# A graph layer on one core: the order of VectorE's two-input operations inside a pass of the main loop

## The chip, the cores and the metric

The kernel runs on 1 core of a Trainium2 chip. The metric is the device time of one execution in microseconds (us). Five engines work side by side, each with its own queue of instructions that it takes strictly in order: PE (TensorE), DVE (VectorE), ACT (ScalarE), POOL (GpSimd) and SP (SyncE, which here only issues transfers).

## The reference

A graph has 12,500 nodes with 128 features each and 200,000 edges (src, dst, weight), sorted by dst. Features are layer-normed and cut at zero. Each edge gets a score from its two ends; each node keeps the 16 edges with the highest scores, and sums their source rows with softmax weights:

```python
h = jnp.maximum(_layernorm(x, axis=-1), 0.0)
Qv = h @ W_Q.T;  Ku = h @ W_K.T
score = einsum('md,md->m', Qv[dst], Ku[src]) / sqrt(d) * exp(-edge_dt)
# rank of each edge among those of its dst, by score
keep = rank < 16
w = where(keep, exp(score - seg_max[dst]), 0)
alpha = w / denom[dst]
agg = segment_sum(alpha[:, None] * (h[src] @ W_msg.T), dst)
out = x + relu(h @ W_self.T + agg)
```

## The kernel before

A first stage norms all rows and writes them to a table in DRAM, h_tab. It also turns the edge lists into columns: idx_all (sources), dec_all (decay), pos_all (an edge's place among those of its node) and dlw (its node, counted from a window's start).

The edges are then cut into G = 112 groups of GC = 14 chunks of 128 edges. A group is worked on with NJ = 15 chunks, since its last node's edges may run into the next group's first chunk. Everything after the first stage happens in one loop, fully written out, with the order of every instruction fixed by hand (tc.manual_schedule): pass i takes one step of several groups at once, each at a different stage. A call at(g, stage) puts a stage of group g in place; what a queue holds follows the order of these calls, and semaphores do the rest.

The life of a group g, with the pass in which each step stands:

- **Gather** (let_go and gather, lines 406 and 395, pass g-2): 14 times, DVE copies two indices from idx_all to ix (line 414) and POOL issues an indirect DMA for each chunk (line 399) that fetches 128 rows of h_tab into hs. POOL does nothing else in the loop. There are 7 hs buffers and 4 of ix. more(k) is let_go for two chunks, k = 0 to 6.
- **places** (line 474, pass g-1, DVE): ow (line 477) marks each edge's node in a window of WN = 40, po (line 479) its slot of KM = 40. Each compares two inputs in SBUF and writes 128 x 600 numbers.
- **far_of, to_edges** (ACT, pass g-1): a matrix from nodes to edges. **q_out, q_parts** (ACT; DVE, line 460, 128 x 128, two inputs in SBUF): the query of each node in three bf16 parts.
- **q_to_edges** (PE, line 490, pass g, in four parts of 4, 4, 4 and 3 chunks; the first stands at the head of the pass) puts the queries on edges, in PSUM; **scores** (DVE, line 500, four parts) multiplies them with the gathered rows and sums, one instruction a chunk. The last chunk of a group is the first of the next one's gather.
- **scores_in_slots** (DVE, line 508, 128 x 600, sl from po and the scores, two inputs in SBUF), at the end of pass g.
- **slots_by_node** (PE, lines 513 and 515, pass g+1), node_by_slots: scores in a node's slots.
- **best** (DVE, lines 529 to 541, pass g+2): the 16 highest per node, some thirteen small operations. It reads the PSUM tile et that slots_by_node of the next group writes too, and stands behind it.
- **kept_to_edges** (PE), **on_edges** (DVE, lines 564 to 571): whether each edge is kept; mine (line 569) has one input in PSUM and one in SBUF.
- **weights** (DVE, pass g+3): kept (line 579) and alz (line 580, 128 x 600, from ow and kept, both in SBUF). **sums** (PE, line 590, two parts) multiplies alz with the gathered rows.
- **sums_turned** (PE, line 598), **products** (PE), **output** (DVE, line 610, pass g+5), **store** (SP). sums_turned writes the PSUM tile so, which output of the group before it reads.

So there are four operations of 128 x 600 with two inputs in SBUF in each pass: sl, alz, ow and po.

Of the kernel before, what the change touches and what calls it, by code (L numbers as in the profile page):

```python
# [58 lines left out]
def bc(ap, n):  # L59

    return ap.unsqueeze(2).to_broadcast([ap.shape[0], ap.shape[1], n])
# [7 lines left out]
def bm(ap, n):  # L69

    return ap.unsqueeze(1).to_broadcast([ap.shape[0], n, ap.shape[1]])
# [3 lines left out]
def gnn_layer(  # L75
# [310 lines left out]
    with tc.tile_pool(name="win", bufs=2) as win, tc.manual_schedule():  # L386
        chunks = [min(NJ, CH - GC * g) for g in range(G)]
# [18 lines left out]
        def let_go(g, k):  # L406

            j0, j1 = 2 * k, min(2 * k + 2, own[g])
            if j0 >= j1:
                return  # L410
            if k == 0:
                T[g]["ix"] = win.tile([P, GC], I32, name="ix", bufs=4)
            ix = T[g]["ix"]
            nc.vector.tensor_copy(ix[:, j0:j1], idx_all[:, GC * g + j0:GC * g + j1])  # L414
            gather(g, j0, j1, lambda j: ix[:, j:j + 1])
# [55 lines left out]
            nc.scalar.activation(T[g]["to_e"][:, 0:n], T[g]["far"][:, 0:n], AF.Relu, bias=1.0, scale=-1.0)  # L471


        def places(g):
            n = chunks[g]
            T[g]["ow"] = win.tile([P, NJ, WN], F32, name="ow", bufs=6)
            nc.vector.tensor_tensor(T[g]["ow"][:, 0:n, :], bm(slots, n), bc(dlw[:, g, 0:n], WN), op=OP.is_equal)
            T[g]["po"] = win.tile([P, NJ, KM], F32, name="po", bufs=5)
            nc.vector.tensor_tensor(T[g]["po"][:, 0:n, :], bm(slots, n),
                                    bc(pos_all[:, GC * g:GC * g + n], KM), op=OP.is_equal)  # L480
# [142 lines left out]
        def at(g, stage, *args):  # L623
            if 0 <= g < G:
                stage(g, *args)
# [4 lines left out]
        for i in range(-3, G + 6):  # L630
            at(i + 3, load_nodes)
            at(i + 2, load_dst)

            more = (lambda k: let_go(i + 2, k)) if 0 <= i < G - 2 else (lambda k: None)
            at(i, q_to_edges, 0)
            at(i - 5, output)
            at(i - 5, store)
            at(i - 3, weights)
            more(0)
            at(i - 4, sums_turned)  # L640
            at(i - 4, sums_turned_out)
            at(i + 1, q_out)
            at(i, q_to_edges, 1)
            at(i + 1, far_of)
            at(i - 1, slots_by_node)
            at(i + 1, places)
            more(1)
            at(i - 2, best)
            more(2)
            at(i - 2, sum_of_exps)  # L650
            at(i - 1, slots_out)
            at(i, q_to_edges, 2)
            at(i + 2, h_turned)
            at(i, scores, 0)
            more(3)
            at(i + 1, to_edges)
            at(i + 1, q_parts)
            at(i + 2, h_turned_out)
            at(i - 3, sums, 0)
            at(i - 2, kept_to_edges)  # L660
            at(i, scores, 1)
            more(4)
            at(i, q_to_edges, 3)
            at(i - 2, one_over_sum)
            at(i - 3, sums, 1)
            at(i, scores, 2)
            at(i - 2, on_edges)
            more(5)
            at(i - 4, products)
            at(i - 3, sums_out)  # L670
            at(i - 2, exps)
            at(i, scores, 3)
            at(i, scores_in_slots)
            more(6)
            at(i - 1, node_by_slots)
            at(i + 2, q_made)

# [180 lines left out]
```

## Time and profile before

| | |
|---|---|
| median of 3 runs | 2125.32 us (2122.5 to 2127.98) |
| the profiled execution: its own time | 2125.5 us |
| its span, first to last instruction | 2123.7 us |
| mean granted TensorE clock | 0.795 |
| busy share: POOL, DVE, PE, ACT | 73%, 70%, 62%, 30% |

The busy share counts an engine's instructions; time in which it issues or waits is left out. The profile comes as a page (busy shares, costliest groups of instructions with what ended the idle time before them) and as answers of the trace: waits, the timeline of an engine, and busy time in chosen stretches. A line as `L477` is line 477 of the kernel, `out<-in` are names of its tiles, and `xcount` is how often.

### The profile page before, as it was taken

What the parts mean: (1) busy time and instruction counts of PE and PEld (TensorE: products, weight loads), DVE (VectorE), ACT (ScalarE), POOL (GpSimd) and SP (SyncE); (2) the same over time, 40 slices, a digit from 0 to 9 for tenths busy, and PEclk for the clock granted to TensorE, in tenths of its full rate; (3) what the DMA queues carried; (4) which work ended last, traced back from release to release, by engine and by line L of the source; (5) the groups of instructions that cost most, each with busy time, mean ns of one, the idle gap of its engine ahead of it and who ended that gap; (6) DMA issues with size and microseconds to landing.
All of it is one profiled execution on the core that took longest, in us unless ns stands there. A gap on an engine that the chain in (4) does not pass through costs nothing. (4 is left out here: it accounts for less than half of the span.)

```text
span 2123.7 us, 43559 instructions
## 1 busy us (share of the span) xinstructions
PE 1312.0 (62%) x14574; PEld 1210.1 (57%) x14575; DVE 1488.2 (70%) x7474; ACT 626.7 (30%) x1225; POOL 1544.1 (73%) x1585
## 2 busy tenths in 40 slices
PE   1166666666666666666666666666666666666665
PEld 1155566555555655555555656565666666565654
DVE  7667677777776777767777767677777776777764
ACT  3442222222222222222222222222222222222220
POOL 1477777777777777777777777777777777777773
PEclk9977877877777877877777777777777787877787
DMA  8453343333343343333333334334433343333420
GB/s 220 146 162 116 119 120 119 120 119 119 120 119 119 116 122 115 115 112 119 118 119 119 119 119 120 119 119 120 120 119 120 119 120 120 119 119 119 120 67 24
DMA packets 118805, 253.18 MB, mean 119 GB/s; under 512 B 33030, under 2 KB 76297, under 8 KB 118558
## 3 DMA queue, kind: packets, MB, share of 16 engines
q1 hardware_dynamic: 67336, 144.92, 19.7%
q0 software_dynamic: 50144, 102.74, 19.1%
q10 hardware_dynamic: 1094, 2.69, 0.5%
q8 instruction: 115, 1.88, 0.4%
q14 instruction: 116, 0.95, 0.1%
HBM read 236.40 MB, written 14.40 MB: 118 GB/s over the span
## 5 line engine op out<-in xcount | busy, mean ns | idle before, releaser
L399 POOL DMA_INDIRECT hs<-h_tab,ix x1535 | 1495.9, 975 | 467.8 <-issue 335.9
L500 DVE SCALAR_TENSOR_TENSOR prod<-hs,dec_all,q 128x128 f32<-128x128 f32 x1674 | 516.9, 345 | 334.3 <-DMA hs<-h_tab,ix 319.1
L490 PE MATMUL q<-q,to_e 128*128 128x128 bf16 x5022 | 464.2, 254 | 33.1 <-DVE prod L500 32.3
L598 PE MATMUL s<-ident,agn 128*128 128x128 f32 x112 | 49.3, 440 | 662.2 <-DVE kept L579 661.7
L490 PEld LDWEIGHTS <-to_e 128*128 128x128 bf16 x5022 | 410.1, 116 | 56.0 <-issue 39.8
L590 PE MATMUL a<-hs,alz 128*128 128x128 f32 x3348 | 425.8, 281 | 0.8 <-DVE alz L580 0.8
L598 PEld LDWEIGHTS s<-ident,agn 128*128 128x128 f32 x112 | 20.2, 180 | 678.4 <-issue 676.7
L590 PEld LDWEIGHTS a<-hs,alz 128*128 128x128 f32 x3348 | 404.4, 197 | 1.2 <-DVE alz L580 1.1
L515 PE MATMUL e<-ow,sl 128*41 128x40 f32 x3348 | 251.3, 265 | 8.4 <-DVE sl L508 8.4
L515 PEld LDWEIGHTS e<-ow,sl 128*41 128x41 f32 x3348 | 235.7, 184 | 23.6 <-DVE sl L508 9.2
L466 ACT ACTIVATE far<-dstb,nb 128x1920 bf16<-128x1920 int32 x112 | 212.9, 1901 | 5.1 <-DMA dstb<-in_dst_dram 5.1
L471 ACT ACTIVATE to_e<-far 128x1920 bf16<-128x1920 bf16 x112 | 201.2, 1796 | 0.1
L602 ACT COPY aggT<-s 128x128 f32<-128x128 f32 x112 | 29.8, 266 | 507.8 <-PE s L598 507.8
L529 DVE TENSOR_SCALAR ell<-slots,e 128x40 f32<-128x40 f32 x112 | 28.3, 253 | 205.3 <-PE e L515 192.6
L546 ACT ACTIVATE e<-v,km 128x16 f32<-128x16 f32 x112 | 34.4, 308 | 363.5 <-DVE km L538 363.5
L500 DVE DVE_READ_ACCUMULATOR prod<-hs,dec_all,q 128x1 f32 x1674 | 139.1, 83 | 0.2
L414 DVE COPY ix<-idx_all 128x2 int32<-128x2 int32 (+1 forms) x768 | 132.7, 173 | 0.0
L575 ACT ACTIVATE up<-up 128x15 f32<-128x15 f32 x112 | 24.1, 215 | 336.5 <-DVE up L567 336.4
L595 ACT ACTIVATE agn<-a,rden 128x128 f32<-128x128 f32 x112 | 41.2, 368 | 209.8 <-PE a L590 209.8
L508 DVE TENSOR_TENSOR sl<-po,s 128x600 f32<-128x600 f32 x112 | 87.5, 781 | 3.9
L580 DVE TENSOR_TENSOR alz<-ow,kept 128x600 f32<-128x600 f32 x112 | 87.5, 781 | 3.8
L399 POOL DMA_INDIRECT hs<-h_tab,idx_all x28 | 33.7, 1203 | 77.6 <-DMA x_end<-zpad 69.4
(150 smaller groups left out, 1562.7 us busy)
## 6 DMA issues: line engine op xcount, KB each, us to landing
dstb<-in_dst_dram SPq DMA_DIRECT2D x111, 960.0 KB
hs<-h_tab,ix POOLq DMA_INDIRECT x1535
h_r<-h_tab SPq DMA_DIRECT2D x112, 64.0 KB
x_t<-in_x_dram SPq DMA_DIRECT2D x108, 64.0 KB
out_dram<-o SPq DMA_DIRECT2D x108, 64.0 KB
xg<-in_x_dram SPq DMA_DIRECT2D x10, 560.0 KB
h_tab<-xg SPq DMA_DIRECT2D x10, 560.0 KB
dst_r<-in_dst_dram ACTq DMA_DIRECT2D x1, 803.2 KB
```

Of the source, the lines that this page charges most:

```text
L399: nc.gpsimd.indirect_dma_start(out=T[g]["hs"][:, j, :], out_offset=None, in_=h_tab[0:N, :], in_offset=bass.IndirectOffsetOnAxis(ap=index(j ...
L414: nc.vector.tensor_copy(ix[:, j0:j1], idx_all[:, GC * g + j0:GC * g + j1])
L466: nc.scalar.activation(T[g]["far"][:, 0:n], T[g]["dstb"][:, 0:n], AF.Square, bias=nb[:, g:g + 1])
L471: nc.scalar.activation(T[g]["to_e"][:, 0:n], T[g]["far"][:, 0:n], AF.Relu, bias=1.0, scale=-1.0)
L490: nc.tensor.matmul(pq[:, (j - j0) * P:(j - j0 + 1) * P], lhsT=T[g]["to_e"][:, j * P:(j + 1) * P], rhs=upper(T[g]["q"][:, k, :]), start=(k ...
L500: nc.vector.scalar_tensor_tensor(prod, rows_of(g, j), dec_all[:, c:c + 1], T[g]["pq", b][:, (j % 4) * P:(j % 4 + 1) * P], op0=OP.mult, op1 ...
L508: nc.vector.tensor_tensor(sl1[g % 2][:, 0:n, 0:KM], T[g]["po"][:, 0:n, :], bc(T[g]["s"][:, 0:n], KM), op=OP.mult)
L515: nc.tensor.matmul(et[0:KM + 1, STEP * j:STEP * j + WN], lhsT=sl1[g % 2][:, j, :], rhs=T[g]["ow"][:, j, :], start=False, stop=(j == n - 1))
L580: nc.vector.tensor_tensor(alz[g % 2].rearrange("e (j w) -> e j w", w=WW + STEP)[:, 0:n, 0:WN], T[g]["ow"][:, 0:n, :], bc(kept[:, 0:n], WN) ...
L590: nc.tensor.matmul(T[g]["pa"][:, 0:P], lhsT=alz[g % 2][:, WW * j + PRE:WW * j + PRE + P], rhs=rows_of(g, j), start=(j == 0), stop=(j == n ...
L595: nc.scalar.activation(T[g]["agn"], T[g]["pa"][:, 0:P], AF.Copy, scale=T[g]["rden"])
L598: nc.tensor.transpose(so[:, 2 * P:3 * P], T[g]["agn"], ident)
```

## The change

Stages of VectorE change their places inside a pass; places is cut into two stages, nodes_of (ow) and places (po). Each stage keeps its pass and its instructions.

```diff
-        def places(g):
+        def nodes_of(g):
             n = chunks[g]
             T[g]["ow"] = win.tile([P, NJ, WN], F32, name="ow", bufs=6)
             nc.vector.tensor_tensor(T[g]["ow"][:, 0:n, :], bm(slots, n), bc(dlw[:, g, 0:n], WN), op=OP.is_equal)
+
+        def places(g):
+            n = chunks[g]
             T[g]["po"] = win.tile([P, NJ, KM], F32, name="po", bufs=5)
...
             at(i - 5, output)
             at(i - 5, store)
-            at(i - 3, weights)
             more(0)
             at(i - 4, sums_turned)
             at(i - 4, sums_turned_out)
...
             at(i, q_to_edges, 1)
             at(i + 1, far_of)
             at(i - 1, slots_by_node)
-            at(i + 1, places)
+            at(i - 2, best)
             more(1)
-            at(i - 2, best)
-            more(2)
+            at(i - 3, weights)
             at(i - 2, sum_of_exps)
             at(i - 1, slots_out)
             at(i, q_to_edges, 2)
             at(i + 2, h_turned)
             at(i, scores, 0)
-            more(3)
+            more(2)
+            at(i + 1, nodes_of)
             at(i + 1, to_edges)
             at(i + 1, q_parts)
             at(i + 2, h_turned_out)
             at(i - 3, sums, 0)
             at(i - 2, kept_to_edges)
             at(i, scores, 1)
-            more(4)
+            more(3)
+            at(i + 1, places)
             at(i, q_to_edges, 3)
             at(i - 2, one_over_sum)
             at(i - 3, sums, 1)
             at(i, scores, 2)
+            more(4)
             at(i - 2, on_edges)
             more(5)
             at(i - 4, products)
             at(i - 3, sums_out)
             at(i - 2, exps)
             at(i, scores, 3)
+            more(6)
             at(i, scores_in_slots)
-            more(6)
```

## The prediction

> **What bounds the kernel now.** I read the page first, then the waits, then the timelines of POOL and VectorE (DVE) over two passes, then busy time by stretches of a pass. The chain that ended last holds only four pieces of the tail and says nothing of the loop. From the page, the groups (count | busy us, mean ns | idle before, releaser):
>
> ```profile
> L399 POOL DMA_INDIRECT hs<-h_tab,ix x1535 | 1495.9, 975 | 467.8 <-issue 335.9 <-DVE prod L500 34.1 <-DMA hs<-h_tab,ix 31.1
> L500 DVE SCALAR_TENSOR_TENSOR prod<-hs,dec_all,q 128x128 f32<-128x128 f32 x1674 | 516.9, 345 | 334.3 <-DMA hs<-h_tab,ix 319.1
> L529 DVE TENSOR_SCALAR ell<-slots,e 128x40 f32<-128x40 f32 x112 | 28.3, 253 | 205.3 <-PE e L515 192.6 <-issue 12.8
> ```
>
> POOL's 1535 gathers take 1495.9 us, and the idle time before them is in small pieces. From the waits (total us, times, longest):
>
> ```profile
> POOL hs L399 <- issue: 343.8, 1128, 0.3
> DVE prod L500 <- DMA hs<-h_tab,ix: 319.1, 399, 2.6
> ```
>
> POOL's longest gap is 0.3 us: it never runs dry. DVE, on the other hand, waits 319 us for gathered rows. So POOL sets the pace, with 14 gathers in a pass. From POOL's timeline (start us, us, engine):
>
> ```profile
> 1004.32 0.94 POOL L399 DMA_INDIRECT hs<-h_tab,ix  x1 [0.30 <-issue]
> 1005.56 1.54 POOL L399 DMA_INDIRECT hs<-h_tab,ix  x1 [0.30 <-issue]
> 1007.41 0.94 POOL L399 DMA_INDIRECT hs<-h_tab,ix  x1 [0.30 <-issue]
> 1024.88 1.08 POOL L399 DMA_INDIRECT hs<-h_tab,ix  x1 [0.30 <-issue]
> ```
>
> An undisturbed gather takes 0.94 and the next starts 0.30 later, so 1.248 a gather and 14 x 1.248 = 17.47 us a pass. Some gathers last longer. DVE's timeline around the first of them:
>
> ```profile
> 1003.18 0.35 DVE L500 SCALAR_TENSOR_TENSOR prod<-hs,dec_all,q 128x128 f32<-128x128 f32 x1 [0.72 <-DMA hs<-h_tab,ix]
> 1003.57 0.79 DVE L508 TENSOR_TENSOR sl<-po,s 128x600 f32<-128x600 f32 x1
> 1004.34 0.28 DVE L610 SCALAR_TENSOR_TENSOR o<-s,x_t 128x128 f32<-128x128 f32 x1
> 1004.74 0.78 DVE L580 TENSOR_TENSOR alz<-ow,kept 128x600 f32<-128x600 f32 x1
> 1005.51 0.78 DVE L477 TENSOR_TENSOR ow<-slots,dlw 128x600 f32<-128x600 f32 x1
> 1006.20 0.78 DVE L479 TENSOR_TENSOR po<-slots,pos_all 128x600 f32<-128x600 f32 x1
> 1009.03 0.25 DVE L529 TENSOR_SCALAR ell<-slots,e 128x40 f32<-128x40 f32 x1 [1.94 <-PE e L515]
> 1010.99 0.16 DVE L414 COPY ix<-idx_all 128x2 int32<-128x2 int32 x1
> 1024.37 0.77 DVE L479 TENSOR_TENSOR po<-slots,pos_all 128x600 f32<-128x600 f32 x1
> ```
>
> The gather at 1005.56 starts 0.05 into ow (L477) and lasts 0.60 too long: it goes on at 1006.16, which is ow's start + 0.65. The one at 1024.88 starts 0.51 into a po (L479), lasts 0.14 too long and goes on at po's start + 0.65. I went through the other long gathers of the loop in the same way: nearly all start inside the first 0.65 us of one of the four 600-element operations with two SBUF inputs (sl, alz, ow, po), and all that start inside it are held to its end. An operation that covers only the later part of a gather costs nothing, and DVE's four are 0.77 to 0.79 whatever POOL does. L569 and L571, as long but with one SBUF input, hold none.
>
> Over 103 passes of the loop the holds are 0.445 us a pass: 65 passes lose 0.5 to 0.7, 32 lose about 0.14 to 0.3, a few others lie between or above. That is all the change can win on POOL: 0.445 x 108 passes = 48 us (the group row gives the same size: 1535 x (975 - 944, the median) = 47.6).
>
> **The change part by part.** No instruction is added or removed. Per pass it moves kept/alz (L579, L580) from before best to behind it, ow (L477) behind scores 0, po (L479) behind scores 1, the second pair of index copies behind best, and the last one ahead of sl. None of it is issued by PE, ACT, SP or POOL, so those four keep their order; the index copies come up to some 4 us later within a pass, but they feed subset i+2 while the rows of subset i are awaited, at least 14 gathers ahead, and POOL does not notice.
>
> DVE's own path. From the output (1004.34) to best (1009.03) is 4.69 us, set by PE: the output frees the bank, then PE runs the transpose, 12 matmuls and slots_by_node. Today 2.76 of it is covered by alz, ow and po; afterwards only by one copy, so best's wait grows from 1.94 to about 4.3. Behind best stands the rest of the pass: best with its copy 2.03, kept and alz 0.90, scores 0 and copy 1.15, ow 0.69, q parts 0.53, scores 1 and copy 1.14, po 0.69, one over the sum 0.26, scores 2 and copy 1.15, on_edges and copy 2.09, scores 3 and copy about 1.0, sl 0.70: 12.3. With 4.69 that is 17.0 a pass, below POOL's 17.47. So DVE's added wait is paid from its waits for rows (3.1 us in the pass shown, about 0.5 to 1 left) and costs nothing; without that cover it would cost 2.4 x 108 = 260 us. PE gets alz about 3 us later relative to the output, waits some 2 us ahead of sums, and still ends about 4 us before the next output, out of the 6 it has.
>
> What decides is therefore where the four operations fall against gathers. The last product of a pass (1003.18) waits for a gathered row and so ties DVE's clock to POOL's in every pass. I walk the new order through the pass shown. sl stays at 1003.57. The output follows it directly, 0.70 later: 1004.27; best 4.69 later: 1008.96; alz after 1.96 + 0.07 + 0.20: 1011.19; ow after 0.70 + 1.08 + 0.07: 1013.04; po after 0.69 + 0.53 + 1.07 + 0.07: 1015.40. Gathers without the old hold start at 1005.57, 1006.82, 1008.06, 1009.31, 1010.56, 1011.81. The last is 0.62 into alz: held 0.03. The next starts at 1013.09, 0.05 into ow: held 0.60. Then 1014.94 and 1016.19, on either side of po. Sum 0.63, where before it was 0.60.
>
> This is no accident of one pass. ow now starts 1.85 after alz, and a gather released by alz starts again 0.65 + 1.248 = 1.90 after alz started, 0.05 into ow; one that just missed alz lands later in ow, by as much. So the pair takes 1.248 minus the gather's place after alz's start, about anything from 0 to 1.25, mean 0.62. With the row arriving 0.07 later against POOL (the passes that now lose only 0.14) the same walk gives 0.70. So with best at 4.69 the holds are about 0.65. Where TensorE's clock rises early, best comes early and each 0.1 us takes 0.1 off: 26 of the 103 passes have best at 4.30 to 4.65 (walk: 0.25 to 0.6). From the busy times by stretch (us, PE, PEld, DVE, ACT, POOL busy, then granted clock, DMA):
>
> ```profile
> 1004.34:1009.03 4.69, 4.26 (x46) 3.82 (x47) 2.72 (x10) 2.23 (x3) 3.78 (x4) 0.50 0.41 107
> 1016.51:1022.50 5.99, 0.00 (x1) 0.00 (x0) 4.24 (x19) 0.21 (x1) 4.47 (x6) 0.79 0.21 55
> ```
>
> PE runs up to best at a granted clock of 0.50, after 6 us of idling; with the idle time split into 2 and 4 the clock may be up in more passes. I take 45 to 75% of the passes at 0.65 and the others at 0.35 to 0.40: 0.51 to 0.575, so 0.545. Against 0.445 that is +0.10 x 108 = +10.8 us on the profiled execution's own 2125.5 (span 2123.7, 1.8 around it; the median of the runs, 2125.32, is the same within 0.2): 2136.
>
> [...]
>
> **The rivals.** *Fewer holds* (faster). The place is the distance from output to best: if PE's clock is up in most passes and its mean falls to 4.44 or less, alz has moved by a quarter and the sum of holds drops below 0.385. For it: PE's long idle time is cut. Against it: 77 of 103 passes now have 4.69, and about 4 us of idling remain. At a mean of 4.2 to 4.3 the holds are 0.15 to 0.25: 2125.5 - 0.245 x 108 = 2099; with none left, 2077.
>
> *The same sum, elsewhere*: holds of 0.39 to 0.50, 2120 to 2131, centre 2125. For it: the walk of the pass shown differs by 0.03 only.
>
> *Two whole holds a pass* (slower by far): best earlier than 4.05, so that alz catches a gather at its beginning and ow another: 0.9 to 1.2, +0.6 x 108, 2190. Or DVE's own 17.0 is short by over a microsecond and binds. Against both: best has not been below 4.29 in these passes, and DVE's parts are all measured.
>
> **How the numbers follow.** Likeliest case (holds 0.50 to 0.75, 2131 to 2158): 0.55. Same sum: 0.20. Fewer holds: 0.18. Two holds or DVE bound: 0.07. A measurement of this kernel tells about 0.3% (6.4 us) from no change, so slower by more is 0.62, within it 0.20, faster 0.18. The range leaves out most of the last case and the far part of fewer holds: 2106 (holds 0.26) to 2162 (holds 0.78).
>
> **What would show it.** Right: L399's mean at 980 to 985 ns instead of 975; long gathers starting inside ow, none inside po; best's wait for L515 up from 193 to over 400 us, products' wait for rows down to about 100; alz starting 7 us after the output. Wrong: a mean near 950 (fewer holds) or over 1000 (two holds); gaps on POOL over 0.3; products that no longer wait for rows (DVE binds).

## The result, and the profile after

The changed kernel takes 2151.64 us (median of 4 runs, 2148.46 to 2154.96), the kernel before 2123.91 beside it: ratio 1.0138, 95% interval 1.0123 to 1.0152. It is slower, as forecast, but by 27.7 us where 10.8 were forecast. The profiled execution took 2151.43, its span is 2149.7: 25.9 us over the span before. (In twelve of the eighteen experiment runs the kernel before, run beside them, itself took 2784 to 2800 us instead of some 2122; these twelve are kept apart below.)

The same three groups of the page as before the change (count | busy us, mean ns | idle before, releaser; lines behind 477 stand three lower in the changed file, so L500 is now L503):

```profile
L399 POOL DMA_INDIRECT hs<-h_tab,ix x1535 | 1514.2, 986 | 467.8 <-issue 316.1
...
L503 DVE SCALAR_TENSOR_TENSOR prod<-hs,dec_all,q 128x128 f32<-128x128 f32 x1674 | 501.4, 344 | 136.8 <-DMA hs<-h_tab,ix 125.5
...
L532 DVE TENSOR_SCALAR ell<-slots,e 128x40 f32<-128x40 f32 x112 | 30.7, 274 | 448.3 <-PE e L518 445.7
```

The gathers' idle time is the same to the digit (467.8) and their busy time is 18.3 us longer. VectorE's waits changed places as forecast: rows 319.1 to 125.5, best 192.6 to 445.7. From the waits (total us, times, longest):

```profile
PE s L601 <- DVE ix L414: 369.3, 105, 5.8
...
POOL hs L399 <- issue: 323.7, 1062, 0.3
...
PE a L593 <- DVE alz L583: 217.1, 112, 3.1
```

POOL's longest gap in the loop is still 0.3: no new wait stands in its way. PE waits about 2 us a pass for alz (217.1 / 112) and still 3.5 for the output (369.3 / 105; the index copy that this row names stands right behind the output, L613). POOL's timeline in two passes:

```profile
1002.98 0.94 POOL L399 DMA_INDIRECT hs<-h_tab,ix  x1 [0.30 <-issue]
1004.23 1.52 POOL L399 DMA_INDIRECT hs<-h_tab,ix  x1 [0.30 <-DVE prod L503]
1006.05 0.94 POOL L399 DMA_INDIRECT hs<-h_tab,ix  x1 [0.30 <-issue]
...
1021.03 0.94 POOL L399 DMA_INDIRECT hs<-h_tab,ix  x1 [0.30 <-issue]
1022.28 1.38 POOL L399 DMA_INDIRECT hs<-h_tab,ix  x1 [0.30 <-DVE ix L414]
```

and VectorE's, of which the two-input operations, the output and the head of best are shown:

```profile
1002.30 0.78 DVE L583 TENSOR_TENSOR alz<-ow,kept 128x600 f32<-128x600 f32 x1
...
1004.15 0.78 DVE L477 TENSOR_TENSOR ow<-slots,dlw 128x600 f32<-128x600 f32 x1
...
1006.52 0.77 DVE L482 TENSOR_TENSOR po<-slots,pos_all 128x600 f32<-128x600 f32 x1
...
1013.52 0.28 DVE L613 SCALAR_TENSOR_TENSOR o<-s,x_t 128x128 f32<-128x128 f32 x1
...
1017.89 0.34 DVE L532 TENSOR_SCALAR ell<-slots,e 128x40 f32<-128x40 f32 x1 [4.01 <-PE e L518]
...
1020.23 0.78 DVE L583 TENSOR_TENSOR alz<-ow,kept 128x600 f32<-128x600 f32 x1
...
1022.07 0.78 DVE L477 TENSOR_TENSOR ow<-slots,dlw 128x600 f32<-128x600 f32 x1
```

In the first pass the gather at 1002.98 starts 0.68 into alz, just past its 0.65, and runs free. The next starts 0.08 into ow and is held to ow's start + 0.65, as before the change: 1004.23 + 1.52 is ow's start + 1.60. In the second, best came 4.37 behind the output instead of 4.69; everything behind it is earlier by as much, so the gather falls 0.21 into ow and is held 0.44. Over the loop ow holds 103 gathers (51.3 us; 67 and 38.1 before), alz 49 (5.9), sl 15 (2.1), and po 4 instead of 36.

Where the 25.9 us stand: the last gather ends at 2103.35 instead of 2085.48, 17.9 later, which is the gathers' longer busy time. The other 8.1 stand in the tail, from there to the end of the span: 46.3 us instead of 38.3. The prediction had nothing there.

### The profile page after: what moved, and what is told of

Same layout as the page of the kernel before. It is cut to its first block, busy times and chain, and to the rows that moved or that the text cites. A ratio compares the mean times of both kernels' runs of the same rounds, so it can differ in the third digit from the quotient of the medians.

```text
span 2149.7 us, 43561 instructions
## 1 busy us (share of the span) xinstructions
PE 1427.9 (66%) x14574; PEld 1307.2 (61%) x14575; DVE 1465.7 (68%) x7474; ACT 624.4 (29%) x1225; POOL 1561.2 (73%) x1585
## 5 line engine op out<-in xcount | busy, mean ns | idle before, releaser
L399 POOL DMA_INDIRECT hs<-h_tab,ix x1535 | 1514.2, 986 | 467.8 <-issue 316.1
L593 PE MATMUL a<-hs,alz 128*128 128x128 f32 x3348 | 531.9, 323 | 217.1 <-DVE alz L583 217.1
L593 PEld LDWEIGHTS a<-hs,alz 128*128 128x128 f32 x3348 | 489.4, 232 | 241.7 <-DVE alz L583 241.7
L503 DVE SCALAR_TENSOR_TENSOR prod<-hs,dec_all,q 128x128 f32<-128x128 f32 x1674 | 501.4, 344 | 136.8 <-DMA hs<-h_tab,ix 125.5
L493 PE MATMUL q<-q,to_e 128*128 128x128 bf16 x5022 | 469.4, 256 | 9.7 <-DVE prod L503 9.6
L493 PEld LDWEIGHTS <-to_e 128*128 128x128 bf16 x5022 | 407.8, 117 | 25.1 <-issue 10.8
L532 DVE TENSOR_SCALAR ell<-slots,e 128x40 f32<-128x40 f32 x112 | 30.7, 274 | 448.3 <-PE e L518 445.7
L601 PE MATMUL s<-ident,agn 128*128 128x128 f32 x112 | 45.5, 406 | 378.7 <-DVE ix L414 369.3
L518 PE MATMUL e<-ow,sl 128*41 128x40 f32 x3348 | 245.3, 262 | 8.3 <-DVE sl L511 8.3
L518 PEld LDWEIGHTS e<-ow,sl 128*41 128x41 f32 x3348 | 229.8, 180 | 23.1 <-DVE sl L511 9.1
L503 DVE DVE_READ_ACCUMULATOR prod<-hs,dec_all,q 128x1 f32 x1674 | 138.3, 83 | 0.2
L399 POOL DMA_INDIRECT hs<-h_tab,idx_all x28 | 33.0, 1178 | 77.9 <-DMA x_end<-zpad 69.7
L574 DVE TENSOR_REDUCE kept<-mine 128x15 f32<-128x600 f32 x112 | 86.9, 776 | 3.8
```

The source lines that it names most:

```text
L399: nc.gpsimd.indirect_dma_start(out=T[g]["hs"][:, j, :], out_offset=None, in_=h_tab[0:N, :], in_offset=bass.IndirectOffsetOnAxis(ap=index(j ...
L493: nc.tensor.matmul(pq[:, (j - j0) * P:(j - j0 + 1) * P], lhsT=T[g]["to_e"][:, j * P:(j + 1) * P], rhs=upper(T[g]["q"][:, k, :]), start=(k ...
L503: nc.vector.scalar_tensor_tensor(prod, rows_of(g, j), dec_all[:, c:c + 1], T[g]["pq", b][:, (j % 4) * P:(j % 4 + 1) * P], op0=OP.mult, op1 ...
L518: nc.tensor.matmul(et[0:KM + 1, STEP * j:STEP * j + WN], lhsT=sl1[g % 2][:, j, :], rhs=T[g]["ow"][:, j, :], start=False, stop=(j == n - 1))
L574: nc.vector.tensor_reduce(kept[:, 0:n], mine[:, 0:n, :], axis=AX.X, op=OP.add)
L593: nc.tensor.matmul(T[g]["pa"][:, 0:P], lhsT=alz[g % 2][:, WW * j + PRE:WW * j + PRE + P], rhs=rows_of(g, j), start=(j == 0), stop=(j == n ...
```

## The experiments

The theory on trial is the prediction's: gathers set the pace, and a two-input operation of VectorE costs as much as the gather that starts inside its first 0.65 us loses. Rivals: VectorE's or TensorE's own path through a pass became longer (the bare wait ahead of best); or it is the distance between the four operations that counts, not their place against gathers.

**Where to read the loop's time.** The profiled execution of each run that could be compared (us):

| kernel | L399 busy (x1535) | last gather ends | tail behind it | span |
|---|---|---|---|---|
| before | 1495.9 | 2085.5 | 38.3 | 2123.7 |
| changed | 1514.2 | 2103.4 | 46.3 | 2149.7 |
| l0, before's order, light TensorE | 1494.7 | 2083.0 | 35.3 | 2118.3 |
| l5, in the gaps, light TensorE | 1455.6 | 2042.4 | 35.2 | 2077.6 |
| e5d, in the gaps | 1455.1 | 2043.4 | 39.8 | 2083.2 |
| e1d, weights back | 1465.3 | 2054.1 | 40.4 | 2094.4 |
| e4b, spare reduce ahead of alz | 1510.6 | 2101.4 | 48.3 | 2149.7 |
| e3b, spare reduce late | 1517.9 | 2106.2 | 49.5 | 2155.7 |

The second column less the first is 587 to 591 us in all eight, while the gathers' busy time covers 63 us and TensorE's work more than a factor of two; the gathers' idle time is 467.7 or 467.8 in each. So up to the last gather, what differs between these kernels is their gathers' own time, and the rest is the tail.

**l0_before_order: is it TensorE?** The order of before, with most of TensorE's products cut to one matmul for each group of them; best then comes 2.63 behind the output instead of 4.63. One of the cuts:

```diff
-            for j in range(n):
-                nc.tensor.matmul(et[0:KM + 1, STEP * j:STEP * j + WN], lhsT=sl1[g % 2][:, j, :],
-                                 rhs=T[g]["ow"][:, j, :], start=False, stop=(j == n - 1))
+            nc.tensor.matmul(et[0:KM + 1, 0:WW], lhsT=upper(sl1[g % 2][:, 0, :]),
+                             rhs=T[g]["to_e"][:, 0:WW], start=True, stop=True)
```

> A base for the runs that follow, the kernel before with TensorE's work cut from some 145 to 12 matmuls a pass (one bf16 matmul for each part of q_to_edges, one for slots_by_node, sums, products, h_turned, two for kept_to_edges, q_made left out), so that the values are no longer those of the layer. Every instruction of VectorE, GpSimd, ScalarE and SyncE and the order of all of them is that of the kernel before. On the chips that serve these calls the kernel before takes 2790 to 2800 us, since TensorE issues single matmuls about 1 us apart while gathers run and POOL waits for it; 12 matmuls a pass leave it room. Theory H: POOL sets the pace again, 14 gathers of 1.248 us and a hold of about 0.45 us a pass, nearly all under ow: 2110 to 2135 us, VectorE waiting for rows in each pass. Rival D (DVE's own path): with TensorE short, DVE's 13.1 us a pass bind: well under 1900. If TensorE's stalls still bind: over 2200, and the base is of no use.

Measured: 2121.47 us beside 2122.65, ratio 0.9995 (0.9986 to 1.0005). From the page (busy us (share) xinstructions, and the gathers):

```profile
PE 515.1 (24%) x1405; PEld 159.6 (8%) x1406; DVE 1490.3 (70%) x7474; ACT 615.4 (29%) x1225; POOL 1543.2 (73%) x1586
...
L401 POOL DMA_INDIRECT hs<-h_tab,ix x1535 | 1494.7, 974 | 467.7 <-issue 318.2
```

TensorE's busy time fell from 1312 to 515 us, and the time stayed. In before's order alz, ow and po stand ahead of best, so best's earlier coming moves none of them, and the holds stay as well (974 ns, 975 before). TensorE is not what the loop waits for.

**l5_in_gaps: the same cut, the four operations put beside gathers' starts.** ow and po go behind the first four of the seven index copies of a pass, with two of the products between them, so that each operation starts shortly after a gather has (e5's order):

```diff
             at(i - 3, weights)
             more(0)
+            more(1)
+            more(2)
+            more(3)
...
-            at(i + 1, places)
-            more(1)
+            at(i + 1, nodes_of)
+            at(i, scores, 0, 0, 2)
+            at(i + 1, places)
             at(i - 2, best)
...
-            at(i, scores, 0)
+            at(i, scores, 0, 2, 4)
```

> The same cut of TensorE's work, with ow and po in the gaps between gather starts (four index copies between alz and ow, two products of scores 0 between ow and po; alz at 1.56, ow at 2.54, po at 3.77 us behind the last product, gather starts at about 2.4, 3.6 and 4.9). Theory H: holds of 0 to 0.05 us a pass instead of about 0.45, so 40 to 50 us below the base with the old order; mean of a gather 945 to 950 ns against about 976. Rival D: the base within 5 us, since DVE's work is the same. Rival A (how far apart the operations stand): the base less 0 to 15 us, since the gaps between three of them are 0.3 to 0.5 us only.

Measured: 2080.07 us beside 2122.65, ratio 0.9804 (0.9788 to 0.9821), and 41.4 below l0; the gathers' mean (L401 there) is 948 ns. The holds are 0.04 us a pass.

**e5d_in_gaps: that order in the whole kernel.**

> The whole layer with ow and po in the gaps between gather starts. Where the kernel before takes about 2123: theory H 2074 to 2090, holds of 0 to 0.05 us a pass; rivals D and A 2110 to 2124. Where the kernel before takes about 2790, TensorE's stalls decide and the time says nothing.

Measured: 2085.69 us beside 2120.81, ratio 0.9836 (0.982 to 0.9853). It beats both kernels, with the same operations. The group of gathers, then VectorE's and POOL's timelines:

```profile
L399 POOL DMA_INDIRECT hs<-h_tab,ix x1535 | 1455.1, 948 | 467.8 <-issue 311.8
```

```profile
1002.15 0.78 DVE L511 TENSOR_TENSOR sl<-po,s 128x600 f32<-128x600 f32 x1
...
1003.37 0.78 DVE L583 TENSOR_TENSOR alz<-ow,kept 128x600 f32<-128x600 f32 x1
...
1004.37 0.77 DVE L477 TENSOR_TENSOR ow<-slots,dlw 128x600 f32<-128x600 f32 x1
...
1005.60 0.77 DVE L482 TENSOR_TENSOR po<-slots,pos_all 128x600 f32<-128x600 f32 x1
```

```profile
1002.87 0.94 POOL L399 DMA_INDIRECT hs<-h_tab,ix  x1 [0.30 <-issue]
1004.11 0.94 POOL L399 DMA_INDIRECT hs<-h_tab,ix  x1 [0.30 <-issue]
1005.36 0.94 POOL L399 DMA_INDIRECT hs<-h_tab,ix  x1 [0.30 <-issue]
1006.61 0.94 POOL L399 DMA_INDIRECT hs<-h_tab,ix  x1 [0.30 <-DVE po L482]
```

The gathers start 0.72 into sl, 0.74 into alz, 0.99 into ow and 1.01 after po began: none in the first 0.65. Each operation lies across the later part of a gather, and none is held; over the loop the holds are 0.06 us a pass. The four stand within 3.45 us, closer than in the changed kernel and nearly as close as before the change (2.63), where they cost 0.445 a pass. So distance between them is not what counts; their place against gathers is.

**e1d_weights_back: one part of the change undone.** In the changed kernel, weights returns to its place behind the output; ow and po stay behind scores 0 and 1.

```diff
             at(i - 5, store)
+            at(i - 3, weights)
             more(0)
...
             at(i - 2, best)
             more(1)
-            at(i - 3, weights)
```

> The changed kernel with kept and alz back behind the output and ow and po left apart behind best. Where the kernel before takes about 2123: theory H 2085 to 2105 (alz at 1.49 and, with best at 4.69, ow at 8.96 and po at 11.33 all miss; passes with an early best lose up to 0.56); rival D 2054 to 2124; rival A 2130 to 2150. Where the kernel before takes about 2790, it says nothing.

Measured: 2092.98 us beside 2120.81, ratio 0.9867 (0.985 to 0.9883): this part of the change alone takes a slowdown of 1.4% to a gain of 1.3%.

```profile
L399 POOL DMA_INDIRECT hs<-h_tab,ix x1535 | 1465.3, 955 | 467.8 <-issue 299.9
```

At the median ow now lies 8.96 behind the last product of a pass and po 11.33, between gathers; both hold almost nothing where best is at 4.69 (0.06 us a pass over 77 passes). Where best comes at 4.25 to 4.5, po catches a gather: 0.66 a pass over 12 passes. The tail, too, returns to 40.4. The time lies in the range of VectorE's path as well (2054 to 2124); against that rival stand e5d, whose path is that of before, and the two runs that follow.

**e4b_spare_early: everything behind best moved by one known step.** The changed kernel with a reduce of 128 x 600 (one input in SBUF) ahead of weights; its result is not used. spare(g) is a tensor_reduce of po(g) over its slots. It moves alz, ow and po by 0.69.

```diff
             more(1)
+            at(i - 2, spare)
             at(i - 3, weights)
```

> The changed kernel with a reduction of 128 x 600 that nothing uses (0.70 us of DVE a pass, one input in SBUF) behind best, ahead of kept and alz. Where the kernel before takes about 2121 and so the changed one about 2149: theory H: alz moves from 8.01 to 8.71 behind the last product and ow from 9.86 to 10.56, so ow catches a gather at its end; holds 0.27 to 0.42 instead of 0.60: 20 to 35 us less, plus 2 us behind the last gather: 2116 to 2132. Rival D (DVE's path): +76, 2225. Rival A (distance between the operations): 2149.

Measured: 2153.21 us beside 2120.35, ratio 1.0165 (1.0135 to 1.0194). The gathers-decide theory had forecast 2116 to 2132: a miss, and by its time alone the run suits the rival of distances (2149). What went wrong shows in the timelines. Stretches from output to best in three passes (us, busy times, then granted clock, DMA share, GB/s):

```profile
1027.94:1032.63 4.69, 4.26 (x46) 3.82 (x47) 0.36 (x3) 2.23 (x3) 3.69 (x4) 0.50 0.47 95
1045.64:1048.57 2.93, 2.50 (x46) 2.29 (x47) 0.36 (x4) 2.16 (x3) 2.32 (x3) 1.00 0.37 99
1064.09:1068.24 4.15, 3.72 (x46) 3.33 (x47) 0.36 (x3) 2.23 (x3) 3.13 (x4) 0.63 0.38 98
```

The same 46 matmuls take 4.26 us at a granted clock of 0.50 and 2.50 at 1.00. The clock was up in many more of these stretches (a mean of 0.66, and 0.57 in the changed kernel): best came at a mean of 4.09 behind the output, at 4.69 in 37 of 101 passes (65 in the changed kernel). That it is PE's idle times, shifted by a still later alz, that raised the clock was not tested. Where it was at 4.69, the step did what the theory said: 0.21 us of holds a pass (walk 0.20), where the changed kernel has 0.70. But the passes at 4.25 to 4.5 lose 1.12 and those below 3 lose 0.99. The second of the three, VectorE first:

```profile
1050.83 0.77 DVE L629 TENSOR_REDUCE junk<-po 128x15 f32<-128x600 f32 x1
1051.71 0.78 DVE L583 TENSOR_TENSOR alz<-ow,kept 128x600 f32<-128x600 f32 x1
...
1053.56 0.78 DVE L477 TENSOR_TENSOR ow<-slots,dlw 128x600 f32<-128x600 f32 x1
```

```profile
1050.59 0.94 POOL L399 DMA_INDIRECT hs<-h_tab,ix  x1 [0.30 <-issue]
1051.83 1.48 POOL L399 DMA_INDIRECT hs<-h_tab,ix  x1 [0.30 <-DVE kept L582]
1053.62 1.53 POOL L399 DMA_INDIRECT hs<-h_tab,ix  x1 [0.30 <-issue]
```

One gather is caught 0.12 into alz, the next 0.06 into ow: two holds in one pass. The reduce holds none: 26 gathers start in its first 0.65 us, and the longest of them lasts 0.95. The walk with each pass's own best gives 0.53 us a pass, 0.57 are measured, correlation 0.99 over 101 passes. So the rule stands, and what failed is the assumption that best's times stay when something else moves. The rival of distances has no reason for holds of 0.21, 1.12 and 0.99 with the distances unchanged. That 0.69 us more on VectorE cost nothing by itself (2153.2 against 2151.6, and 0.69 x 108 would be 75) speaks against VectorE's path as the bound.

**e3b_spare_late: the same reduce where products that wait for rows follow it.** It stands behind more(5).

```diff
             more(5)
+            at(i - 2, spare)
             at(i - 4, products)
```

> The changed kernel with the same reduction behind on_edges, ahead of scores 3, after all four operations with two inputs. Where the kernel before takes about 2121: theory H: DVE has 1.1 us a pass of waiting for rows to pay it from, and nothing moves against the gathers: 2149 to 2155. Rival D: +76, 2225. Rival A: 2149.

Measured: 2158.27 us, ratio 1.0173 (1.0153 to 1.0193). The theory's range ended 3 us lower; VectorE's own path as the bound would have given 2225. The gathers are 3.7 us longer than in the changed kernel, 3.4 of it under sl (5.9 instead of 2.5 us over the whole run), which the expectation had put at nothing. The tail is 3.2 longer, which is about the price of the reduce in the last passes (four times 0.7 to 0.8), where no gather covers it.

**e6_old_order_at_end: the tail.** The changed kernel, with before's order of stages in the last passes, from pass 109 on.

```diff
+            late = i >= G - 3
...
             at(i - 5, store)
+            if late:
+                at(i - 3, weights)
...
-            at(i - 3, weights)
+            if not late:
+                at(i - 3, weights)
```

(and nodes_of, places likewise)

> The changed order, but from pass 109 on (no gather is left to issue in the last three groups' passes) the stages stand as in the kernel before. POOL and its holds stay as in the changed kernel. Gathers-decide theory: the last gather ends as in the changed kernel (2103 us), but the tail behind it shortens from 46 to about 38 us, since weights stands behind the output again instead of behind best when nothing but DVE's and PE's own chain sets the end: 8 us below the changed kernel, 2141 to 2145 where the kernel before takes 2122. Rival (the whole +26 us comes from the loop, by holds or by DVE's longer path, and the tail is paid elsewhere): within 3 us of the changed kernel, 2148 to 2152.

Measured: 2910.5 us beside 2798.14 of the kernel before, so the time decides nothing. The expectation was also wrong that no gather is left from pass 109 on: pass 109 still lets go the last nine. But its trace behind the last gather can be read. VectorE in a late pass of the kernel before, from one output to the next:

```profile
2090.31 0.28 DVE L610 SCALAR_TENSOR_TENSOR o<-s,x_t 128x128 f32<-128x128 f32 x1
2090.71 0.78 DVE L580 TENSOR_TENSOR alz<-ow,kept 128x600 f32<-128x600 f32 x1
...
2098.10 0.29 DVE L610 SCALAR_TENSOR_TENSOR o<-s,x_t 128x128 f32<-128x128 f32 x1 [0.21 <-PE s L606]
```

the same pass of the changed kernel:

```profile
2111.32 0.29 DVE L613 SCALAR_TENSOR_TENSOR o<-s,x_t 128x128 f32<-128x128 f32 x1 [0.84 <-PE s L609]
...
2113.16 0.25 DVE L532 TENSOR_SCALAR ell<-slots,e 128x40 f32<-128x40 f32 x1 [1.55 <-PE e L518]
...
2115.32 0.78 DVE L583 TENSOR_TENSOR alz<-ow,kept 128x600 f32<-128x600 f32 x1
...
2122.27 0.29 DVE L613 SCALAR_TENSOR_TENSOR o<-s,x_t 128x128 f32<-128x128 f32 x1 [0.63 <-PE s L609]
```

and of e6:

```profile
2872.39 0.28 DVE L613 SCALAR_TENSOR_TENSOR o<-s,x_t 128x128 f32<-128x128 f32 x1
2872.78 0.78 DVE L583 TENSOR_TENSOR alz<-ow,kept 128x600 f32<-128x600 f32 x1
...
2874.90 0.25 DVE L532 TENSOR_SCALAR ell<-slots,e 128x40 f32<-128x40 f32 x1 [1.33 <-PE e L518]
...
2880.06 0.29 DVE L613 SCALAR_TENSOR_TENSOR o<-s,x_t 128x128 f32<-128x128 f32 x1 [0.20 <-PE s L609]
```

alz comes 4.0 us behind the output in the changed kernel and 0.4 in the other two, and the next output 10.95 against 7.79 and 7.67. Before the change, the three passes from the output at 2078.19 on took 12.1, 7.8 and 6.0 us; in the changed kernel 15.1, 11.0 and 7.6; in e6 11.1, 7.7 and 6.0. From the last sl to the end of the span it is 33.9, 39.7 and 34.1. Nothing is gathered there any more, so a late alz has no cover. e2 (below), the kernel before with weights alone moved behind best, shows the same:

```profile
2721.26 0.29 DVE L610 SCALAR_TENSOR_TENSOR o<-s,x_t 128x128 f32<-128x128 f32 x1 [0.18 <-PE s L606]
...
2725.28 0.78 DVE L580 TENSOR_TENSOR alz<-ow,kept 128x600 f32<-128x600 f32 x1
...
2732.24 0.29 DVE L610 SCALAR_TENSOR_TENSOR o<-s,x_t 128x128 f32<-128x128 f32 x1 [0.20 <-PE s L606]
```

From its last sl to the end it is 42.2. In all sixteen traces with TensorE's whole work this stretch takes 32.9 to 36.0 where alz follows the output (ten) and 39.7 to 42.3 where it follows best (six). e1d, which has weights back in every pass, gives the price in a comparable run: its tail is 40.4, so 6.0 of the 8.1 go with the place of weights. The other 2.1 lie within what early-alz orders of the whole kernel differ by (38.3, 39.8 and 40.4).

**The runs whose time decides nothing.** The kernel before took 2784 to 2800 us beside these. In their own traces POOL stands idle between gathers for some 230 to 835 us more than in the runs of the table above, so holds, some 120 us at most, do not set their time:

| run | edit | us | before beside it |
|---|---|---|---|
| e1_weights_back, e1b, e1c | as e1d | 2895.2, 2895.8, 2893.2 | 2799, 2790, 2791 |
| e2_only_weights | before, weights alone behind best | 2763.9 | 2799 |
| e3_spare_late | as e3b | 2921.1 | 2799 |
| e4_spare_early | as e4b | 2866.4 | 2799 |
| e5_in_gaps, e5b, e5c | as e5d | 2942.1, 2941.0, 2926.0 | 2790, 2795, 2784 |
| la_after_order, la2_after_order | changed order, light TensorE | 2400.7, 2418.6 | 2784, 2798 |

What was expected of them, edit by edit. Weights back (e1_weights_back, then the repeats):

> The changed kernel with one part undone: kept and alz (weights) stand behind the output again, ahead of best; ow and po stay apart, behind scores 0 and scores 1. Theory H (POOL sets the pace, a gather is held when its start falls into the first 0.65 us of an operation with two inputs in SBUF, and where those fall is fixed by the last product that waits for a row): counted from that product, alz starts at 1.49, ow at 8.96, po at 11.33; gathers start at about 1.13, 8.62 and 9.86, 11.11 and 12.36, so all three miss when best comes 4.69 us after the output. Only passes in which best comes early lose up to 0.56. Holds 0.07 to 0.18 us a pass instead of 0.60 after and 0.45 before: 2085 to 2100 us, faster than both kernels. Rival D (DVE's own longer path with the bare wait ahead of best binds): that wait shrinks by 0.9 us a pass, 2151.6 - 0.9 x 108 = 2054 if all of it counted, at most back to about 2124 if POOL takes over. Rival A (operations that stand apart each find a gather of their own): between the two kernels, 2130 to 2150.

> The changed kernel with kept and alz (weights) back behind the output, once more beside the kernel before on whatever chip serves this call; in the call before, the kernel before itself took 2799 us and TensorE's sums, not POOL, set the pace. Where the kernel before takes about 2124, theory H expects 2085 to 2100, rival D 2054 to 2124, rival A 2130 to 2150, as written for the first run of it. The long gathers that are left should start under po, in passes in which best comes early.

> The changed kernel with kept and alz (weights) back behind the output, one look, to see whether POOL sets the pace again on this chip. Where the kernel before takes about 2124, theory H expects 2085 to 2100 (mean of a gather 948 to 956 ns), rival D 2054 to 2124, rival A 2130 to 2150, as written before.

The spare reduce, late and early:

> The changed kernel with one more operation on DVE in each pass, whose result nothing uses: a reduction of 128 x 600 with one input in SBUF (0.70 us to the next start), between on_edges and scores 3, behind all four operations with two inputs. Theory H: DVE still waits 1.1 us a pass for rows, so this is covered and nothing moves against the gathers: 0 to +4 us (the passes after the last gather), 2151 to 2156. Rival D (DVE's path binds): +0.70 x 108 = +76, about 2227. Rival A: no change.

> The changed kernel with the same spare reduction of 0.70 us in each pass, but put ahead of kept and alz, behind best. Theory H: alz moves from 8.01 to 8.71 behind the last product, just past the gather that it now catches at its end, and ow from 9.86 to 10.56, so that ow catches a gather at its end (0.10) instead of its beginning (0.60). Walked over the changed kernel's own passes the holds become 0.27 to 0.42 a pass instead of 0.60: the added work makes the kernel faster by 20 to 35 us, less 2 us after the last gather: 2118 to 2134. In passes with an early best the hold is about 1. Rival D: +76, about 2227. Rival A (distances between the operations stay, so the holds stay): 2152.

In the gaps (e5_in_gaps, then the repeats):

> The kernel before with ow and po put where theory H sees no gather start: all four operations with two inputs stay within 4.5 us of the last product that waits for a row, alz at 1.56 as before, then four index copies instead of one, ow at 2.54, two products of scores 0, po at 3.77, best after that as before (5.85). Gathers start at about 2.25 to 2.43, 3.50 to 3.68 and 4.75: none falls into the first 0.65 us of alz, ow or po. Theory H: holds fall from 0.45 to 0.00 to 0.03 a pass, so 2124 - 0.43 x 108 = 2077, 2074 to 2086, the mean of a gather 946 to 949 ns; everything else as before. Rival D (DVE's own path and the wait ahead of best bind): the path and the wait are those of before, so 2124. Rival A (what counts is how far apart the operations stand): two of the three gaps are 0.3 to 0.5 us, so little changes: 2110 to 2124.

> The kernel with ow and po put into the gaps between gather starts, once more, beside the kernel before alone. In the two calls before, the kernel before took 2790 to 2800 us: TensorE issued single matmuls 0.7 to 1.4 us apart for long stretches of each pass, and POOL waited for other engines, so the holds decided nothing there. Where the kernel before takes about 2124, theory H expects 2074 to 2086, with a mean gather of 946 to 949 ns and no hold under ow or po; rival D 2124; rival A 2110 to 2124.

> The whole layer again (nothing left out), with ow and po in the gaps between gather starts, on whatever chip serves this call. Where the kernel before takes about 2123, theory H expects 2074 to 2090, as in the pair with little TensorE work (2121 to 2080), holds of 0 to 0.05 us a pass, a mean gather of 946 to 950 ns; rivals D and A 2110 to 2124. Where the kernel before takes about 2790, TensorE's stalls decide and this says nothing.

All four edits missed their numbers here, against the theory as against the rivals. Where the kernel before took its usual time they met or nearly met them (e1d, e3b, e5d), or missed them for the reason told (e4b).

Two edits were never run in a comparable setting. la, the changed order with l0's cuts, was to set best's time to one early value in every pass:

> The same cut of TensorE's work as in the base, with the changed kernel's order. In the base best starts 2.63 us after the output in every pass instead of 4.69, since TensorE is short. Theory H, walked with 2.63: counted from the last product, alz starts at 5.95 and catches the gather of 5.79 + its hold early, for 0.4 to 0.6, and ow at 7.80 catches the next for 0.60: holds of 1.0 to 1.2 us a pass instead of 0.43, so 0.6 to 0.7 x 108 above the base's 2121: 2185 to 2200, with half of the holds under alz and half under ow. Here the holds are far larger than in the changed kernel itself (0.60), though VectorE has more time. Rival D (the wait ahead of best binds): that wait is 2 us a pass shorter than in the changed kernel, so the loss shrinks, to 2121 to 2130. Rival A (distance between the operations alone): as in the changed kernel, +27: 2148.

> The changed order with most of TensorE's products left out (12 matmuls a pass remain), so that best comes 2.6 us behind the output in nearly every pass, whatever the clock. Gathers-decide theory: the walk with 2.63 in place of 4.69 gives 1.08 us of holds a pass against 0.43 of the order before with the same cut (2121): 2185 to 2200, slower than the changed kernel though TensorE has next to nothing to do. Rival (DVE's or PE's own path is what became longer): faster than the changed kernel, 2080 to 2125. Rival (distance between the operations alone counts, not their place against the gathers): as the changed kernel, 2145 to 2155.

and e2 was to do the move of weights alone:

```diff
             at(i - 5, store)
-            at(i - 3, weights)
...
             at(i - 2, best)
             more(2)
+            at(i - 3, weights)
```

> The kernel before with one part of the change: only kept and alz (weights) move behind best; ow and po stay side by side ahead of best. Theory H: counted from the last product, ow starts at 1.43 and misses, po at 2.12 holds the gather that starts near 2.37 for 0.40, alz at about 8.08 mostly misses (gathers near 7.75 and 9.0) unless best is early. Holds 0.40 to 0.50 a pass, as before (0.45); the passes after the last gather get longer as in the changed kernel (+8 us there): 2124 to 2137. Rival D: best's bare wait grows by 0.9 us of the 2.4, so a third of the loss or more: 2135. Rival A: alz alone is set apart: 2130 to 2145. This run tells little between them by its time; by its trace, H wants the long gathers under po and none under ow.

Their times say nothing of the theory: e2's ratio of 0.9859 is one against a kernel that ran some 675 us longer than it does otherwise, and in la2 best came at a mean of 1.7 instead of 2.6, with POOL idle for long stretches. In e2's trace the long gathers stand under po (105) and not under ow (2), as expected, but also under alz (107), where few were expected.

The rule of single gathers can be read in all twenty traces, these twelve among them. Of 2852 gathers of the loop that start in the first 0.65 us of one of the four operations, 2838 last, within 0.03 us, until that operation's start + 1.595, or the undisturbed time if that is longer. Of the 26,229 others 189 last over 0.04 us too long: six start 0.02 to 0.05 us ahead of ow, and 183 stand at q_parts, a fifth operation with two inputs in SBUF, but of 128 x 128. Most of these are e2's (105), with 0.1 us each: one starts 0.06 into q_parts and lasts 1.04.

## Why the prediction was right in direction and short in size

- **POOL sets the pace; no gap opens on it.** Right: idle 467.8 in both, gaps 0.3 at most, and the table of eight kernels.
- **The rule of the holds.** Right: long gathers inside ow (103), almost none inside po (4), and three other orders whose holds went where the rule puts them.
- **VectorE's bare wait ahead of best is covered.** Right in the loop: best's wait 445.7 (over 400 forecast), rows 125.5 (about 100 forecast), and e4b added 0.69 us a pass for next to nothing.
- **The places of the operations.** Right: at the median alz starts 8.02 behind the last product, ow 9.86, po 12.23, which is where the walk puts them (1011.19, 1013.04 and 1015.40 less 1003.18: 8.01, 9.86, 12.22). L399's mean was forecast at 980 to 985 ns and is 986.
- **The size of the holds: too small.** Forecast 0.545 us a pass, measured 0.596. The share of passes with best at 4.69, 45 to 75%, was a choice from one row of the clock; 65 of 101 lies inside it, which is in part luck. They were put at 0.65 and lose 0.70, the upper of the two walks that the prediction made; the others were put at 0.35 to 0.40 and lose 0.41: 0.64 x 0.05 + 0.36 x 0.04 is the missing 0.05. Over the loop that is +0.15 a pass instead of +0.10, so 16 us; with the passes before and behind the window that was counted, the gathers' 18.3.
- **The tail: no term at all.** The step that failed is "PE gets alz about 3 us later relative to the output ... and still ends about 4 us before the next output". That slack exists while gathers pace the loop. In the last passes they do not, and the late alz is paid: the tail grew by 8.1 us, of which weights' return gives back 6.0 (e1d). On the profiled executions 25.9 us were measured and 10.8 forecast; of the 15.1 that were missing, the tail is 8.1 and the later end of the last gather the other 7.1. The trace of before showed these passes (outputs 7.8 and 6.0 apart instead of 17.9), and nothing in the sum asked what the moved step costs there.
- **Fewer holds** did not come: best at a mean of 4.46, just above the 4.44 from which that rival began. But its price, one tenth off for each 0.1 us, was wrong too. Best is 0.23 earlier than 4.69 at the mean, and the holds are 0.596, not some 0.42; the 26 passes with best at 4.25 to 4.5 still lose 0.49. In e4b best came much earlier and the holds were still 0.57, because an earlier best shifts operations out of one gather and into the next.
- **Two whole holds** for a best earlier than 4.05 did not come either: in the changed kernel eight passes have best at 2.9, and they lose 0.22 each, not 0.9 to 1.2. In e4b, with alz 0.69 later, passes with the same best lose 0.99. So best's time alone does not give the holds.

## What to carry to other kernels

In these runs POOL set the pace and four instructions of VectorE held it, and what decided was where each of the four started against a gather, not how far they stood apart: within 3.45 us they cost 0.06 us of holds a pass in e5d, within 2.63 us 0.445 before the change. In a kernel of that kind, put such instructions just behind a start of the pacing one, and behind something whose time is tied to the pacing engine, not to a clock that rises and falls (in e4b, best came 4.69 us behind the output in a stretch at 0.50, and 2.93 in one at 1.00). Then cost a moved step twice, once in the loop, where slack covers it, and once in the passes that drain it, where nothing does (here 6.0 us of the tail).

## What was not expected of the hardware

- What a hold depended on: the first 0.65 us of an operation of 128 x 600 with two inputs in SBUF (2838 of the 2852 gathers above), about 0.15 of one of 128 x 128 (in the kernel before, four of the five gathers that start 0.04 to 0.12 into q_parts last 0.982 to 1.055, the fifth 0.949, undisturbed ones 0.944), and none of a 600-element operation with one input in PSUM (in the changed kernel 96 gathers start in the first 0.65 us of mine, L572; the longest lasts 0.95). Only the head counted: in e5d the four operations begin while a gather runs, and the holds are 0.06 us a pass; the six gathers that start 0.02 to 0.05 us ahead of ow are the exception. No run shows why.
- The granted clock acted on POOL's time through two other engines: 46 matmuls in 4.26 or 2.50 us (granted clock 0.50 and 1.00) shifted VectorE's operations by up to 1.76 us, and a pass of e4b then lost 0.2 or 1.1 us on gathers, of some 18. Every record of the granted clock is 0.50 or 1.00 in e4b, as in the kernel before (222 records) and the changed one (338); the stretch at 0.63 holds both. What decides between the two was not tested.
- In two of the runs beside which the kernel before took 2784 to 2800 us, e5 and e6, the trace shows TensorE issuing matmuls one at a time in places. In e5, eleven single ones start 0.72 to 1.43 us apart, from 1019.61 to 1029.65. Its timeline in e6:

```profile
1511.17 0.28 PE L518 MATMUL e<-ow,sl 128*41 128x40 f32 x1 [0.31 <-issue]
1511.89 0.22 PE L518 MATMUL e<-ow,sl 128*41 128x40 f32 x1 [0.44 <-issue]
1512.60 1.54 PE L518 MATMUL e<-ow,sl 128*41 128x40 f32 x19 [0.48 <-issue]
```

  Three starts lie 0.71 to 0.72 apart, with no wait on another engine; the 19 behind them take 1.54 together. Behind the last gather, e6's passes take what the kernel before takes (7.7 and 6.0 us), so there it was seen only while gathers ran. What causes it was not found.
